# Attention and feed-forward layer on one core: the output product in three float32r passes, the softmax division on ScalarE, evictions without a buffer between

## The chip, the cores and the metric

The kernel runs on one core of a Trainium2 chip. The metric is the device time of one execution in microseconds; three runs of the kernel before gave 1560.99, 1563.09 and 1563.77 us, so the median is 1563.09 us. A core has five engines that run beside each other, each with its own in-order queue: TensorE (PE in the profile, with its weight loads as PEld), VectorE (DVE), ScalarE (ACT), GpSimd (POOL) and SyncE (SP), which here issues all transfers. Matmul results land in PSUM, in tiles of one bank each; only VectorE and ScalarE take them out ("evict" them) here.

## The reference

All arrays are float32. `x` is (2, 1024, 512), there are 16 heads of width 128, and the hidden layer has 1365 columns.

```
def attn(x):                                  # 16 heads, d_head 128, causal
    q, k, v = (einsum('bsd,hed->bhse', x, W) for W in (W_Q, W_K, W_V))
    scores = einsum('bhse,bhme->bhsm', q, k) / sqrt(128)
    pattern = softmax(where(causal, -1e9, scores))
    z = einsum('bhsm,bhme->bhse', pattern, v)
    return einsum('bhse,hde->bsd', z, W_O)    # the output product
def ffn(x):                                   # w1, w3, w2 rounded to three values
    return einsum('bsh,dh->bsd', silu(x @ w1q.T) * (x @ w3q.T), w2q)
x = x + layernorm(attn(layernorm(x)))
x = x + layernorm(ffn(layernorm(x)))
```

## The kernel before, in words

**Number formats.** TensorE is used in two ways. A float32 matmul is one instruction in the program and leaves two records in the profile. A float32r matmul takes operands of reduced width and leaves one record. The projections to query, key and value keep float32 accuracy with float32r: each operand is split into three forms, `lead` (the value scaled and cut to float32r), `low` (what is left) and `diff`, and a product is made of three passes: lead by lead and low by low go to one PSUM tile (`main`), the form `diff` by `diff` to a second one. `combine` (L414) then computes `main * (T12 + 1) - diff` with T12 = 4096. Weights arrive raw and are split on the core: `lead_and_low` (L394, ScalarE and GpSimd) and `difference_form` (L403, VectorE). Scores (L509), values (L572) and the output product (L478) use plain float32 matmuls.

**Loops.** The attention walks over 32 heads `n` (16 for each of two batches). Two heads make a pair `g` with `j` = 0 (even head) and 1 (odd head). Each head has eight steps `i`, one for each tile of 128 queries. In a step the main loop (L658 to L727) records, in this order: filler matmul groups from a table `fill`, the values of a finished block of two query tiles (`values`, L562), weight preparation, and the scores and softmax of the query tile that is three steps ahead (`look`, `AHEAD = 3`). The fillers are: query and key projections of the next head in steps 3 to 6; value projections of the next pair in steps 0, 1, 5 and 7 of odd heads; and in even heads the eight output units of the pair before (`output_units`, L472), one for each tile of 128 tokens, at steps 0, 1, 1, 3, 5, 7, 7, 7.

**Softmax of a tile** (`scores`, L504): matmuls to `s_ps` (two buffers), causal minimum and negated maximum on VectorE (L514, L518), exponent with row sum on ScalarE (L525), reciprocal on VectorE (L530), multiplication by it on VectorE (L531), two copies that separate the 16-bit halves on GpSimd (L536), a transposing transfer (L541), and, a step or more later, a copy to `pt` on VectorE (`join`, L557). Then `values` multiplies `pt` with `v_sb`, and ScalarE copies the result to `zT` (L579).

**PSUM.** Four banks (`ps_m`) serve projections, values, output units, transposes and the hidden layer in turn; two tiles of two banks (`ps_s`) serve the scores. An output unit takes one `ps_m` tile and two matmuls, and VectorE adds it to `acc` (L486; the first pair of a batch copies it, L484).

**What sets the order.** A scheduler turns the recorded order into one queue for each engine. `behind(...)` and `issue_after` hold marked work back until a named instruction has been placed. An engine never passes an instruction that waits.

**The end of the attention.** In the last head (n = 31) the fillers are four output units of the pair before, four `split_unit`s (L222, they load, normalise, transpose and split a tile for the feed-forward part) and two early hidden tiles of the feed-forward part (`early_hidden`, L645, `EARLY = 2`). After it come the last two values blocks and the last eight output units. `zL0` and `zL1` are separate buffers for the last pair. Then the feed-forward part runs hidden tiles (L285) and the product back (L765), and `load_t13` and `load_t2` fetch its weights; most of these weights lie where attention tiles lay.

Of the kernel before, what the change touches and what calls it, by code (L numbers as in the profile page):

```python
# [35 lines left out]
def sandwich_kernel(  # L36
# [16 lines left out]
    NC = D // P  # L53
    NT = S // P
    KB = 256
    QB = 512
# [248 lines left out]
    with ExitStack() as att:  # L305
# [5 lines left out]
        vpool = att.enter_context(tc.tile_pool(name="v", bufs=2))  # L311
        zpool = att.enter_context(tc.tile_pool(name="z", bufs=1))
        tpool = att.enter_context(tc.tile_pool(name="t", bufs=2))
        qpool = att.enter_context(tc.tile_pool(name="q", bufs=2))
# [61 lines left out]
        def load_raw(kind, n):  # L376

            if kind == 2:
                w, src = wpool.tile([P, NC, 2 * P], FP, name="wv", tag="vd"), wv[n % NP]
            else:  # L380
                w = wpool.tile([P, NC, P], FP, name="wqk", tag=("qd", "kd")[kind])
                src = (wq, wk)[kind][n % (2 * NP)]
            nc.sync.dma_start(w, src)
            wraw[kind, n] = w

        def load_output(g, tag):
            weights[3, g] = w = wpool.tile([P, 2, D], FP, name="wo", tag=tag)
            nc.sync.dma_start(w, wo[g % NP])

        def form(kind, name):  # L390
            shape = [P, NC, 2 * P if kind == 2 else P]
            return wpool.tile(shape, FR, name="qkv"[kind] + name)

# [20 lines left out]
        def combine(dst, main, diff, scale, shaped=lambda ps: ps):  # L414
            held = tpool.tile([P, TB], FP, name="held")
            nc.scalar.mul(held, main, scale * (T12 + 1.0))  # L416
            if scale == 1.0:
                nc.vector.tensor_tensor(
                    dst, shaped(held), shaped(diff), ALU.subtract
                )  # L420
            else:
                nc.vector.scalar_tensor_tensor(
                    dst, shaped(diff), -scale, shaped(held), ALU.mult, ALU.add
                )
# [47 lines left out]
        def output_units(g):  # L472
            b, pr = divmod(g, NP)

            def unit(t):
                ps = ps_m.tile([P, TB], FP, name="mm")
                for j in range(2):
                    nc.tensor.matmul(  # L478
                        ps, lhsT=zs[g, t // QT][:, j, ts(t % QT, P)],
                        rhs=weights[3, g][:, j, :],  # L480
                        start=(j == 0), stop=(j == 1),
                    )
                if pr == 0:
                    nc.vector.tensor_copy(acc[:, t, :], ps)  # L484
                else:
                    nc.vector.tensor_tensor(acc[:, t, :], ps, acc[:, t, :], ALU.add)  # L486

            return [lambda t=t: unit(t) for t in range(NT)]
# [15 lines left out]
        def scores(n, i):  # L504
# [25 lines left out]
            nc.vector.reciprocal(ri, rs)  # L530
            nc.vector.tensor_scalar(p_sb[:, :L], p_sb[:, :L], ri, None, ALU.mult)  # L531

# [29 lines left out]
        def values(n, m):  # L562

            g, j = divmod(n, 2)
            qb, half = divmod(m, 2)
            if j == 0 and half == 0:
                name = f"zT{qb}" if g < G - 1 else f"zL{qb}"
                zs[g, qb] = zpool.tile([P, 2, QB], FP, name=name)
            ps = ps_m.tile([P, TB], FP, name="mm")
            for kt in range(2 * m + 2):  # L570
                c0 = max(0, kt - 2 * m) * P
                nc.tensor.matmul(  # L572
                    ps[:, c0:KB],
                    lhsT=proj[g, 2][:, kt, ts(j, P)],
                    rhs=pts[n, m][:, kt, c0:KB],
                    start=(kt == 0),
                    stop=(kt == 2 * m + 1),
                )
            nc.scalar.copy(zs[g, qb][:, j, ts(half, KB)], ps[:, :KB])  # L579

# [61 lines left out]

        EARLY = 2

        def early_hidden(f):  # L645
            def pair():
                return [wpool.tile([P, TB], FR, name="qk"[f] + n) for n in "al"]

            hidden(0, 0, f, lambda: tpool.tile([P, TB], FP, name="held"), pair)

# [7 lines left out]
        for n in range(N):  # L658
# [18 lines left out]
            if j == 0 and g > 0:  # L677
                outs = output_units(g - 1)
                put((0, 1, 1, 3, 5, 7, 7, 7) if g < G - 1 else (0, 1, 3, 7), outs)
            if n == 2 * (NP - 1):  # L680
                units = [lambda t=t: block_unit(1, t) for t in range(NT)]
                put((4, 5, 5, 6, 6, 6, 7, 7), units)
            if n == 2 * NP + 1:
                put(sorted(2 * list(range(NT))), middle_units(0, xpool))
            if n == N - 1:
                splits = [lambda t=t: split_unit(0, 0, t, xpool) for t in range(QT)]
                put((0, 1, 2, 3), splits)
                put((1, 2, 3, 4), outs[QT:])
                put((6, 7), [lambda f=f: early_hidden(f) for f in range(EARLY)])
            for i in range(NT):  # L690
                idx = n * NT + i
                with behind("turn", of=idx + 1):
                    if n + 2 < N and i > 5:
                        load_raw(i - 6, n + 2)
                    if j == 0 and g + 1 < G and i == 1:
                        load_raw(2, g + 1)
                    if j == 1 and g < G - 1 and i == 2:
                        load_output(g, "wo")
                    if n == N - 1 and i == 0:
                        load_output(g, "vl")  # L700
                    if n == N - 1 and i < EARLY:
                        name = ("va", "vd")[i]
                        load_t13(i, wpool.tile([P, 2, D], FR, name=name))
                todo = fill[i]
# [7 lines left out]
                with behind("max", "half", "exp", of=idx + 1):  # L712
                    if n + 1 < N and i in (2, 3):
                        difference_form(i - 2, n + 1, EVERY)
                    if n + 1 < N and i in (1, 2):
                        lead_and_low(i - 1, n + 1, EVERY)
                    if j == 0 and g + 1 < G and i in (3, 4):
                        lead_and_low(2, g + 1, (FRONT, BACK)[i - 3])
                    if j == 0 and g + 1 < G and i in (5, 6):
                        difference_form(2, g + 1, (FRONT, BACK)[i - 5])  # L720
                look(idx + AHEAD)
# [12 lines left out]
    with ExitStack() as ffn:  # L734
# [6 lines left out]

        load_t13(EARLY, wpool.tile([P, 2, D], FR, name="wo"))
        t2 = [tpool.tile([P, D], FR, name=f"t2_{f}") for f in range(NF)]
# [70 lines left out]
        for f in range(NF):  # L814
            load_t2(f)
            if f > EARLY:
                load_t13(f, tpool.tile([P, 2, D], FR, name=f"t13_{f}"))
        middle = middle_units(1, xpool)
        for n, (b, tb, f) in enumerate(steps):
# [5 lines left out]
            if end and f == NF - 4:  # L825
                ffn_hidden(*steps[n + 2])
                ffn_hidden(*steps[n + 3])
            elif n + 2 < len(steps) and not (end and f == NF - 3):
                ffn_hidden(*steps[n + 2])
# [55 lines left out]
```

## Time and profile before

| | |
|---|---|
| median of three runs | 1563.09 us |
| profiled execution, its own time | 1561.59 us |
| its span (first to last instruction) | 1559.8 us |
| granted TensorE clock | 0.994 |
| output product (L478), 512 records | 232.6 us busy |
| softmax multiplication on VectorE (L531), 256 | 138.1 us busy |
| eviction copies to `held` on ScalarE (L416), 192 | 113.7 us busy |
| adding output units to `acc` (L486), 112 | 74.7 us busy |
| attention, about | 0 to 1311 us of the span |

Busy times are the union of an engine's records, so a busy engine may still have work that is stretched or pipelined: the records of matmuls that follow each other overlap, and the time from one start to the next is shorter than a record. For the cost of a matmul the length of a run of equal matmuls, divided by their number, is what counts. A "wait" names the engine and line that waited, what ended the wait, the sum in us, how often, and the longest. In the table of stages each engine has its busy time and, in brackets, its instructions.

### The profile page before, as it was taken

The page shows a single profiled execution, that of the slowest core. Times are in us where ns is not written, and L with a number is a line of the kernel's source. Part 1 is how long each engine was busy: PE and PEld are TensorE (multiplying, and loading weights), DVE is VectorE, ACT ScalarE, POOL GpSimd, SP SyncE. Part 2 cuts the span into 40 slices and gives each one's busy share as a digit, 9 for nine tenths or more (in the row PEclk, how much of TensorE's full clock was granted, in tenths as well). Part 3 has the DMA queues.
Part 4 walks back from the last instruction along what each step waited for, and adds up shares of the span by engine and source line. Part 5 has one row for each costly group of instructions (what it writes and reads, how often), then busy time and mean ns, then how long its engine had stood idle before and what let it go on. Part 6 is the DMA issues. An engine that isn't in the chain of part 4 may idle for free. (4 is left out here: it accounts for less than half of the span.)

```text
span 1559.8 us, 20141 instructions
## 1 busy us (share of the span) xinstructions
PE 1523.6 (98%) x6822; PEld 1143.9 (73%) x6822; DVE 1129.5 (72%) x2115; ACT 538.3 (35%) x1116; POOL 574.0 (37%) x685
## 2 busy tenths in 40 slices
PE   5999999999999999999999999999999999999997
PEld 4876868686868686677677777777777776888885
DVE  5787777777777878789887777777777784744343
ACT  4332323333334334333333333333333341433333
POOL 4434343433333546544454444444453330010010
PEclk9999999999999999999999999999999999999999
DMA  2374555555545455556655555555554476110100
GB/s 88 80 151 111 113 108 114 112 115 107 121 105 124 98 124 122 131 115 158 169 115 115 115 115 115 115 115 115 108 102 88 75 167 195 55 55 0 41 28 27
DMA packets 357615, 164.91 MB, mean 106 GB/s; under 512 B 311092, under 2 KB 324404, under 8 KB 357512
## 3 DMA queue, kind: packets, MB, share of 16 engines
q1 hardware_dynamic: 357512, 163.62, 45.8%
q8 instruction: 54, 0.88, 0.2%
q14 instruction: 49, 0.40, 0.1%
HBM read 73.39 MB, written 14.68 MB: 56 GB/s over the span
## 5 line engine op out<-in xcount | busy, mean ns | idle before, releaser
L536 POOL COPY half<-p_sb 128x640 uint16<-128x640 uint16 (+7 forms) x512 | 343.8, 700 | 712.9 <-DVE p_sb L531 371.7
L525 ACT ACTIVATE p_sb<-s_ps,nm 128x128 f32<-128x128 f32 (+7 forms) x256 | 189.9, 742 | 591.9 <-DVE nm L518 570.6
L509 PE MATMUL s_ps<-k,q 128*128 128x512 f32 (+3 forms) x768 | 290.1, 486 | 0.3 <-ACT p_sb L525 0.3
L572 PE MATMUL mm<-pt,v_sb 128*128 128x256 f32 (+1 forms) x1280 | 272.4, 360 | 5.9 <-DVE pt L557 3.5
L572 PEld LDWEIGHTS mm<-pt,v_sb 128*128 128x128 f32 x1280 | 239.9, 191 | 47.5 <-issue 8.2
L557 DVE COPY pt<-halfT 128x256 uint16<-128x256 uint16 (+7 forms) x256 | 248.2, 970 | 3.1 <-DMA halfT<-half 3.1
L478 PE MATMUL mm<-wo,zT 128*128 128x512 f32 x480 | 218.7, 592 | 0.0
L509 PEld LDWEIGHTS s_ps<-k,q 128*128 128x128 f32 x768 | 132.6, 191 | 92.4 <-issue 86.2
L518 DVE TENSOR_REDUCE nm<-s_ps 128x1 f32<-128x128 f32 (+7 forms) x256 | 193.5, 756 | 7.3
L514 DVE TENSOR_TENSOR s_ps<-s_ps,causal 128x128 f32<-128x128 f32 x256 | 75.6, 295 | 147.3 <-PE s_ps L509 147.1
L459 PE MATMUL mm<-va,xb 128*128 128x256 f32 x512 | 158.3, 309 | 0.0
L478 PEld LDWEIGHTS mm<-wo,zT 128*128 128x128 f32 x480 | 90.6, 189 | 92.3 <-issue 79.7
L416 ACT ACTIVATE held<-mm 128x512 f32<-128x512 f32 x192 | 113.7, 592 | 101.0 <-PE mm L459 66.1
L531 DVE TENSOR_SCALAR p_sb<-p_sb,ri 128x128 f32<-128x128 f32 (+7 forms) x256 | 138.1, 539 | 10.0 <-DVE ri L530 0.5
L459 PE MATMUL mm<-vd,xb 128*128 128x256 f32 x512 | 144.9, 283 | 0.3 <-DVE acc L486 0.3
L459 PE MATMUL mm<-vl,xb 128*128 128x256 f32 x512 | 144.6, 282 | 0.0
L285 PE MATMUL mm<-xb,t 128*128 128x512 f32 (+1 forms) x512 | 122.5, 392 | 0.0
L435 PE MATMUL mm<-xb,qa 128*128 128x512 f32 x256 | 120.9, 472 | 1.4 <-ACT xb L365 1.4
L435 PE MATMUL mm<-xb,ka 128*128 128x512 f32 x256 | 112.6, 440 | 0.0
L285 PEld LDWEIGHTS mm<-xb,t 128*128 128x128 f32 (+1 forms) x512 | 93.0, 183 | 21.4
L435 PE MATMUL mm<-xb,ql 128*128 128x512 f32 x256 | 102.9, 402 | 2.5 <-DVE xb L367 2.5
L459 PEld LDWEIGHTS mm<-vl,xb 128*128 128x128 f32 x512 | 97.8, 191 | 6.7 <-issue 3.6
(127 smaller groups left out, 2171.7 us busy)
## 6 DMA issues: line engine op xcount, KB each, us to landing
wqk<-wq SPq DMA_DIRECT2D x32, 256.0 KB, 3.5
wqk<-wk SPq DMA_DIRECT2D x32, 256.0 KB, 3.4
wv<-wv SPq DMA_DIRECT2D x16, 512.0 KB, 3.9
wo<-wo SPq DMA_DIRECT2D x16, 512.0 KB, 3.9
xt<-x SPq DMA_DIRECT2D x32, 256.0 KB, 3.2
raw<-w SPq DMA_DIRECT2D x30, 256.0 KB, 3.3
tern<-raw SPq DMA_DIRECT2D x30, 256.0 KB, 2.7
t<-tern SPq DMA_DIRECT2D x24, 256.0 KB, 5.5
```

The costliest lines, as they stand in the source:

```text
L285: nc.tensor.matmul(ps[:fl, :], lhsT=t[:, c, :], rhs=bl[k][:, c, :], start=(c == 0 and k == 0), stop=(c == NC - 1 and k == 1),)
L416: nc.scalar.mul(held, main, scale * (T12 + 1.0))
L435: nc.tensor.matmul(main, lhsT=forms[f][0][:, c, :], rhs=forms[f][1][:, c, :], start=(c == 0 and f == 0), stop=(c == NC - 1 and f == 1),)
L459: nc.tensor.matmul((main, main, diff)[f][:, ts(t, 2 * P)], lhsT=forms[f][0][:, c, token], rhs=forms[f][1][:, c, :], start=(t == 0 and c == ...
L478: nc.tensor.matmul(ps, lhsT=zs[g, t // QT][:, j, ts(t % QT, P)], rhs=weights[3, g][:, j, :], start=(j == 0), stop=(j == 1),)
L509: nc.tensor.matmul(s_ps[:, ds(k0, kl)], lhsT=proj[n, 0, i // QT][:, ts(i % QT, P)], rhs=proj[n, 1, k0 // TB][:, :kl], start=True, stop=True,)
L518: top = nc.vector.tensor_reduce(nm, s_ps[:, :L], axis=AX.X, op=ALU.max, negate=True)
L525: e = nc.scalar.activation(p_sb[:, :L], s_ps[:, :L], AF.Exp, bias=nm, accum_out=rs)
L531: nc.vector.tensor_scalar(p_sb[:, :L], p_sb[:, :L], ri, None, ALU.mult)
L536: copy = nc.gpsimd.tensor_copy(half[:, ds(k * L, L)], words[:, :L, k])
L557: nc.vector.tensor_copy(words[:, 0 : i + 1, :, ts(il, P)], turned[:, 0 : 2 * (i + 1), :].rearrange("p (k t) q -> p t k q", k=2),)
L572: nc.tensor.matmul(ps[:, c0:KB], lhsT=proj[g, 2][:, kt, ts(j, P)], rhs=pts[n, m][:, kt, c0:KB], start=(kt == 0), stop=(kt == 2 * m + 1),)
```

## The change

It does the following.

- **Output product.** `values` no longer copies `z` once. It writes three float32r forms of it: `lead` on ScalarE, `low` on VectorE (both read PSUM) and `diff` on GpSimd. The weights W_O are loaded raw like the value weights (`load_raw` kind 3), regrouped on the host, and split on the core in steps 3 to 6 of odd heads. An output unit is six float32r matmuls to two `ps_m` tiles, `main` and `diff`, and two VectorE instructions: `acc = main * (T12 + 1) + acc`, then `acc = acc - diff`. (The first pair of a batch does the first of the two on ScalarE.)
- **Buffers.** `zT` and `zL` give way to four rotating buffers of each form (`ZB = 4`).
- **Softmax.** The multiplication by the reciprocal goes from VectorE to ScalarE.
- **Evictions.** `combine` lets ScalarE write `main` straight to the destination, and VectorE subtracts `diff` in place; the tile `held` and its pool go.
- **End of the attention.** All output units of pair 14 stand in head 30. Three of the four splits move from head 31 to steps 5 to 7 of head 30. Three hidden tiles instead of two (`EARLY = 3`) stand in steps 2, 4 and 6 of head 31; their weights are loaded in head 30. In the feed-forward part the weights of hidden tiles 5 to 7 go to the buffers of W_O's forms.

```diff
         def combine(dst, main, diff, scale, shaped=lambda ps: ps):
-            held = tpool.tile([P, TB], FP, name="held")
-            nc.scalar.mul(held, main, scale * (T12 + 1.0))
+            nc.scalar.mul(dst, shaped(main), scale * (T12 + 1.0))
             if scale == 1.0:
-                nc.vector.tensor_tensor(
-                    dst, shaped(held), shaped(diff), ALU.subtract
-                )
+                nc.vector.tensor_tensor(dst, dst, shaped(diff), ALU.subtract)
...
             def unit(t):
-                ps = ps_m.tile([P, TB], FP, name="mm")
-                for j in range(2):
-                    nc.tensor.matmul(
-                        ps, lhsT=zs[g, t // QT][:, j, ts(t % QT, P)],
-                        rhs=weights[3, g][:, j, :],
-                        start=(j == 0), stop=(j == 1),
-                    )
-                if pr == 0:
-                    nc.vector.tensor_copy(acc[:, t, :], ps)
-                else:
-                    nc.vector.tensor_tensor(acc[:, t, :], ps, acc[:, t, :], ALU.add)
+                main, diff = (ps_m.tile([P, TB], FP, name="mm") for _ in range(2))
+                for f in range(3):
+                    for j in range(2):
+                        nc.tensor.matmul(
+                            (main, main, diff)[f],
+                            lhsT=zs[g, t // QT, j][f][:, ts(t % QT, P)],
+                            rhs=weights[3, g][f][:, 2 * j : 2 * j + 2, :],
+                            start=(j == 0 and f != 1),
+                            stop=(j == 1 and f > 0),
+                        )
+                dst = acc[:, t, :]
+                if pr == 0:
+                    nc.scalar.mul(dst, main, T12 + 1.0)
+                else:
+                    nc.vector.scalar_tensor_tensor(
+                        dst, main, T12 + 1.0, dst, ALU.mult, ALU.add
+                    )
+                nc.vector.tensor_tensor(dst, dst, diff, ALU.subtract)
...
             nc.vector.reciprocal(ri, rs)
-            nc.vector.tensor_scalar(p_sb[:, :L], p_sb[:, :L], ri, None, ALU.mult)
+            nc.scalar.mul(p_sb[:, :L], p_sb[:, :L], ri)
...
-            nc.scalar.copy(zs[g, qb][:, j, ts(half, KB)], ps[:, :KB])
+
+            lead, low, diff = (w[:, ts(half, KB)] for w in zs[g, qb, j])
+            nc.scalar.mul(lead, ps[:, :KB], LEAD / T12)
+            nc.vector.scalar_tensor_tensor(
+                low, lead, -T12, ps[:, :KB], ALU.mult, ALU.add
+            )
+            nc.gpsimd.tensor_tensor(diff, lead, low, ALU.subtract)
...
-        EARLY = 2
+        EARLY = 3
...
             if j == 0 and g > 0:
                 outs = output_units(g - 1)
-                put((0, 1, 1, 3, 5, 7, 7, 7) if g < G - 1 else (0, 1, 3, 7), outs)
+                put((0, 1, 1, 3, 5, 7, 7, 7), outs)
...
+            splits = [lambda t=t: split_unit(0, 0, t, xpool) for t in range(QT)]
+            if n == N - 2:
+                put((5, 6, 7), splits)
             if n == N - 1:
-                splits = [lambda t=t: split_unit(0, 0, t, xpool) for t in range(QT)]
-                put((0, 1, 2, 3), splits)
-                put((1, 2, 3, 4), outs[QT:])
-                put((6, 7), [lambda f=f: early_hidden(f) for f in range(EARLY)])
+                put((0,), splits[3:])
+                put((2, 4, 6), [lambda f=f: early_hidden(f) for f in range(EARLY)])
...
-                    if j == 1 and g < G - 1 and i == 2:
-                        load_output(g, "wo")
+                    if j == 1 and i == 1:
+                        load_raw(3, g)
...
-                    if j == 0 and g + 1 < G and i in (3, 4):
-                        lead_and_low(2, g + 1, (FRONT, BACK)[i - 3])
-                    if j == 0 and g + 1 < G and i in (5, 6):
-                        difference_form(2, g + 1, (FRONT, BACK)[i - 5])
+                    at = g + 1 - j
+                    if at < G and i in (3, 4):
+                        lead_and_low(2 + j, at, (FRONT, BACK)[i - 3])
+                    if at < G and i in (5, 6):
+                        difference_form(2 + j, at, (FRONT, BACK)[i - 5])
```

## The prediction

> **What bounds the kernel now.** I read the page's busy shares first, then the stages, the chain that ended last, the groups with their idle times, and VectorE's timeline inside one even head. The page:
>
> ```profile
> PE 1523.6 (98%) x6822; PEld 1143.9 (73%) x6822; DVE 1129.5 (72%) x2115; ACT 538.3 (35%) x1116; POOL 574.0 (37%) x685
> ```
>
> A busy PE need not stream at its full rate, so the chain that ended last, with runs of equal matmuls:
>
> ```profile
> 787.83 5.15 PE mm L478 x12
> ...
> 1287.03 4.24 DMA halfT<-half
> 1292.66 5.20 PE mm L572 x16
> 1297.86 13.73 PE mm L478 x32
> 1311.59 3.67 PE mm L285 x16
> 1317.08 3.63 PE mm L285 x16
> ```
>
> L478 is the output product in float32: 13.73 / 32 = 0.429 us for each record of 512 columns, two records for each matmul. L285 is float32r at 512 columns with a fresh stationary operand each time: 3.65 / 16 = 0.228 us. In the middle of the attention the output units run at the same 5.15 / 12 = 0.429, so there TensorE streams without holes. The stages agree (two odd and two even heads in turn):
>
> ```profile
> 950.00:989.00 39.00, 39.00 (x211) 32.10 (x211) 28.04 (x54) 13.64 (x30) 16.09 (x20) 1.00 0.54 129
> 989.00:1028.00 39.00, 39.00 (x142) 25.68 (x141) 32.36 (x58) 12.05 (x28) 19.96 (x22) 1.00 0.47 102
> 1028.00:1067.00 39.00, 39.00 (x212) 32.12 (x211) 27.98 (x53) 13.75 (x30) 16.09 (x20) 1.00 0.55 124
> 1067.00:1106.00 39.00, 39.00 (x142) 25.73 (x141) 32.68 (x58) 12.05 (x28) 19.97 (x22) 1.00 0.47 101
> ```
>
> After the span the columns are PE, PEld, DVE, ACT, POOL. TensorE bounds both kinds of head; VectorE is second, with 28.0 us in an odd head and 32.4 in an even one, where the output units stand. The groups that the change touches:
>
> ```profile
> L478 PE MATMUL mm<-wo,zT 128*128 128x512 f32 x480 | 218.7, 592 | 0.0
> L486 DVE TENSOR_TENSOR acc<-mm,acc 128x512 f32<-128x512 f32 x112 | 74.7, 682 | 25.6 <-PE mm L478 25.4
> L422 DVE SCALAR_TENSOR_TENSOR q<-mm,held 128x512 f32<-128x512 f32 x64 | 43.6, 681 | 3.2 <-PE mm L440 3.2
> L407 DVE SCALAR_TENSOR_TENSOR vd<-vl,va 128x512 fp32r<-128x512 f32 x32 | 24.4, 764 | 2.4 <-POOL vl L401 2.4
> L531 DVE TENSOR_SCALAR p_sb<-p_sb,ri 128x1024 f32<-128x1024 f32 x32 | 23.9, 748 | 1.0
> L525 ACT ACTIVATE p_sb<-s_ps,nm 128x1024 f32<-128x1024 f32 x32 | 35.8, 1118 | 89.7 <-DVE nm L518 89.7
> ```
>
> **The change part by part.**
>
> *Output product on TensorE.* Removed: 128 units x 4 records x 0.429 = 219.6 us. Added: 128 x 6 x 0.228 = 175.1. Gain 44.5 us, all on the path, because L478 waits for nothing (0.0 idle) and the stages are full. Bounds: 3.63 and 3.67 us per 16 give 45.3 and 43.5. The Trainium skill ("FP8 and Floating Point Precision", TensorE Precision Notes) counts four passes for true float32, and "TensorE: Matmul & The Clock Gate" (Back-to-back issue gap) gives about 216 ns for a warm 512-column pass; four passes to three would then give an estimated 128 x 2 x 0.216 = 55 us. The float32r rows here run at 0.228, and the sum keeps 44.5.
>
> *VectorE, even heads.* Each unit now needs two evictions of about 0.68 us (rows L422, L486) where it needed one: +8 x 0.68 = 5.4 us a head. The low form of z is new, four a head, 256 columns out of PSUM; no row has it. Between 295 ns for 128 columns (L514, 75.6 us over 256) and 681 for 512 I take 0.42: +1.7. The softmax multiplication goes: 138.1 us over 32 heads, -4.3. So 32.4 + 2.8 = 35.2 us of VectorE against 39.0 - 8 x 0.348 = 36.2 of TensorE: 97%. *Odd heads:* -4.3, +1.7, and two half forms of W_O at 0.764: 28.0 - 1.1 = 26.9 of 39.0, with room.
>
> What does 97% cost? A unit fills two of the four `ps_m` banks instead of one, so a late VectorE stops TensorE sooner: three units at step 7 take six banks. VectorE's idle time in the even head from 989 to 1028 us is mostly waiting for TensorE:
>
> ```profile
> 993.39 0.30 DVE L514 TENSOR_TENSOR s_ps<-s_ps,causal 128x128 f32<-128x128 f32 x1 [1.35 <-PE s_ps L509]
> ...
> 1008.41 0.30 DVE L514 TENSOR_TENSOR s_ps<-s_ps,causal 128x128 f32<-128x128 f32 x1 [0.49 <-PE s_ps L509]
> ...
> 1026.34 0.69 DVE L486 TENSOR_TENSOR acc<-mm,acc 128x512 f32<-128x512 f32 x1 [0.77 <-PE mm L478]
> ...
> 1028.06 0.69 DVE L486 TENSOR_TENSOR acc<-mm,acc 128x512 f32<-128x512 f32 x1 [1.02 <-PE mm L478]
> ```
>
> Together 6.3 us, of which 0.75 waits for ScalarE's row sums. Waits for TensorE vanish when VectorE is late, so VectorE needs between 35.2 + 0.75 = 35.95 us (nothing lost against 36.2) and 35.2 + 6.3 = 41.5 (5.3 lost). Below nothing cannot be, since TensorE's own work takes the 36.2. At steps 1 and 2 the even head is tight already: from 993.39 VectorE has eleven us of work in a row. Laying the new order on these durations, the values group after the pair of units waits about 0.3 us for the first unit's bank, 0.9 when the slow form of L207 (1.68 us) lies before it; the triple just fits. I take 0.6 us for each of 15 even heads: **+9 us** (0 to 80), nearer the low end because nearly all of that idle time is TensorE's.
>
> *Middle of the kernel.* From 720 to 800 us the row statistics of batch 0 come on top: VectorE 70.6 of 80, PE idle 2.3. The two later even heads get the same load plus 2.8 us: **+2.5** (0 to 6).
>
> *Softmax division on ScalarE.* Priced by the exponent of the same width (1118 ns for 1024, 189.9 us over all 256), ScalarE goes from 538 to about 538 + 190 + 20 (leads of W_O, 32 x 0.62) + 10, half of the span. The chain of a tile gets longer by 1.118 - 0.748 = 0.37 us, by one eviction of 0.59 queued between exponent and product, and by GpSimd, which gets 128 z differences (half of L371's 1417 ns, 0.7 each) and 32 halves of W_O (1.35 each, L401). Cover: the copy to `pt` waits for its transfer only 3.1 us in the whole run, so the transposed tile lies ready and VectorE's turn gates it; I take **+2** (0 to 32: the fourth values block of each of 32 heads starts only some 1.5 us after its copy, and would pay about 1 us). Were that cover gone, values wait and all later PE work with them. "VectorE: DVE Perf Modes" (The perf-mode tier table) speaks against this move: one-source float32 work between SBUF tiles runs there at twice the normal rate, which agrees with 748 against 1118 ns. By that rule alone the move loses an estimated 52 us of engine time; by the stages it takes VectorE's 4.3 us a head away where they are scarce.
>
> *Evictions without `held`.* Same instructions, same durations: nothing. ScalarE must now find the destination free; its last reader (scores at the latest in step 4) precedes the projection on PE's own queue.
>
> *z in three forms, W_O on the core.* ScalarE's lead replaces the copy (370 ns). Transfers: one of 512 KB for each pair as before, a step earlier, on SP before a transposition; it waits for the last reader of the form whose buffer it takes, done a step before. Nothing, covered by two steps (9 us) before its use.
>
> *End of the attention.* Four units, three splits and their loads leave head 31, a hidden tile enters; TensorE's total is unchanged. Left behind the last score are 3.66 + 1.51 + 2.38 = 7.5 us of PE work instead of 11.2 (two hidden tiles, two values blocks), while the softmax of the last tile takes the same 14.5 us (from about 1278.1 to 1292.66). It loses the splits that held VectorE (a load from `mid` on the chain at 1270.96) and gains about 1 us on ScalarE, where the activation-table load and the SiLU of the third hidden tile stand before its product. The hole before the last values block, 3.2 us, becomes about 7: **+4** (0 to 8). The last eight units take 8 x 1.36 us of VectorE plus row statistics (0.69 each) against 11.0 of TensorE: **+1** (0 to 3). Six loads of hidden weights now wait behind those units on SP; they are needed 12 us later: nothing.
>
> Sum: -44.5 + 9 + 2.5 + 2 + 4 + 1 = -26 us. The profiled execution took 1561.6 us, 1.5 under the median, so it would take 1535.6; against the median I say **1537 us**.
>
> **The rivals.**
> - *Everything is hidden* but the end: 1563.1 - 44.5 + 3 = 1521. For it: VectorE's idle time is TensorE's. Against: 97% in lumps.
> - *Values wait for the longer softmax chain.* The 32 fourth blocks pay 1 us: 1537 - 2 + 32 = 1567; half of them, 1552. For it: 1.5 us of slack. Against: 3.1 us of transfer waits.
> - *VectorE becomes the bound of the even heads; the kernel gets slower.* If all 6.3 us of idle time stay, an even head takes 41.5 instead of 39.0: 15 x 2.5 = +38, less 2.8 for the last units, plus 9.5 of the other terms: 1608. It decides when a head loses over (44.5 - 9.5) / 15 = 2.3 us, so when 3.3 of the 6.3 us stay. For it: four banks, two for each unit. Against: an odd head has 12 us of room to catch up.
> - *The passes are no cheaper* with z as a fresh stationary operand: the pass would have to take 0.286 us. Against: L285 loads one for each pass too, in 188 ns beside the matmul.
>
> **How the numbers follow.** Main case (1526 to 1549) 0.60; all hidden (1517 to 1526) 0.13; values wait in part (1549 to 1562) 0.12; values wait fully, VectorE bound, or passes no cheaper (over 1562) 0.15. Range 1518 to 1564 leaves out some 0.02 below and 0.14 above. A measurement of this kernel tells 0.2%, 3 us, from no change: faster 0.84, the same 0.02, slower 0.14.
>
> **What would show it.** In the profile after: L473 pitch 0.228 us; even heads about 36.8 us long, odd ones 39; VectorE near 35 us in an even head; waits of PE on VectorE's evictions (L484, L487, z low) of about 10 us in all; a hole of some 7 us before the last values block. Wrong if waits of the values on `pt` appear in bulk, if an even head is longer than 39 us, or if ScalarE's product is late because evictions before it wait for TensorE.

## The result, and the profile after

The changed kernel is slower by 0.5%: 1569.62 us (1568.53 to 1570.43 in five runs) against 1562.2 us (1560.5 to 1563.77 in five), a ratio of 1.0047, 95% interval 1.0032 to 1.0062. The forecast was 1537 us, with 1564 as its upper end and a chance of 0.14 for slower.

At first sight the page after contradicts this. Here it is, engine by engine (busy us, share of the span, instructions):

```profile
PE 1493.4 (95%) x7078; PEld 1192.4 (76%) x7078; DVE 1177.0 (75%) x2131; ACT 745.4 (48%) x1424; POOL 733.3 (47%) x845
```

TensorE is busy for 30 us less than before, and the span is 8 us longer (1567.6 against 1559.8). So TensorE's work shrank and it waits more. Its work is close to the forecast: from start to start a pass of L473 takes 0.229 us (median of 768), and the sum of all matmuls, each at the median of its kind, fell from 1507.4 to 1465.4 us, by 42. The same sum of the gaps that really passed rose from 1540.5 to 1547.1. The difference of the two sums is time beyond the usual pitch: 33 us before, 82 after. So some 49 us of new waiting stand against 42 us of saved work.

The groups of after that answer to those shown of before (after the bar: busy us in all and mean ns of one, then the engine's idle time just before them and what ended it):

```profile
L473 PE MATMUL mm<-oa,za 128*128 128x512 f32 x256 | 95.5, 454 | 5.8 <-DVE acc L484 5.6 <-DVE acc L487 0.2
L473 PE MATMUL mm<-ol,zl 128*128 128x512 f32 x256 | 79.8, 393 | 0.0
L484 DVE SCALAR_TENSOR_TENSOR acc<-mm,acc 128x512 f32<-128x512 f32 x112 | 74.2, 681 | 0.8
L582 DVE SCALAR_TENSOR_TENSOR zl<-za,mm 128x256 fp32r<-128x256 f32 x128 | 53.5, 418 | 79.1 <-ACT za L581 78.7
L585 POOL TENSOR_TENSOR zd<-za,zl 128x256 fp32r<-128x256 f32 x128 | 112.4, 878 | 83.9 <-DVE zl L582 60.3 <-ACT p_sb L526 15.0 <-DMA halfT<-half 5.1
L558 DVE COPY pt<-halfT 128x2048 uint16<-128x2048 uint16 x32 | 52.8, 1651 | 1.1 <-DMA halfT<-half 1.1
L208 DVE SCALAR_TENSOR_TENSOR raw<-raw,scales,tmp 128x512 f32<-128x512 f32 x30 | 40.8, 1359 | 12.7 <-POOL tmp L204 12.7
L532 ACT ACTIVATE p_sb<-p_sb,ri 128x1024 f32<-128x1024 f32 x32 | 36.9, 1152 | 29.6 <-DVE ri L531 29.3
```

The new instructions cost what was estimated (0.681 us an eviction, 0.418 a low form, 1.152 for the widest division, priced at 1.118). Two old ones grew that the change does not touch: the widest copy to `pt` from 1387 to 1651 ns, the ternary difference L208 (L207 before) from 987 to 1359 ns. The kernel before:

```profile
L557 DVE COPY pt<-halfT 128x2048 uint16<-128x2048 uint16 x32 | 44.4, 1387 | 2.9 <-DMA halfT<-half 2.9
L207 DVE SCALAR_TENSOR_TENSOR raw<-raw,scales,tmp 128x512 f32<-128x512 f32 x30 | 29.6, 987 | 3.9 <-POOL tmp L203 3.9
```

And VectorE now waits 78.7 us for ScalarE's lead form of z. The list of waits shows who is late (us in all, times, longest). The kernel after:

```profile
DVE zl L582 <- ACT za L581: 78.7, 92, 6.9
DVE s_ps L515 <- PE s_ps L510: 25.2, 42, 2.6
PE mm L572 <- DVE acc L484: 14.5, 10, 4.0
PE mm L572 <- DVE pt L558: 7.2, 3, 3.4
```

The kernel before:

```profile
DVE s_ps L514 <- PE s_ps L509: 147.1, 139, 2.9
PE mm L572 <- DVE pt L557: 3.5, 2, 3.2
```

Before, VectorE waited 147.1 us for the scores; now 25.2, so it is late in many places, and TensorE's values group L572 waits for its evictions. Summed over the run by the engine that ended them, VectorE's waits for TensorE fell from 279 to 123 us, but those for ScalarE rose from 97 to 192 and those for GpSimd from 10 to 31. (A lead of z can be written only when its values group is done: of the 79 us of idle time ahead of L582, 23 pass before TensorE has ended that group.)

A stage table of one even and one odd head (from the fourth score tile of a head to that of the next; columns as before, at the end the granted clock, the DMA share and GB/s). The kernel before:

```profile
992.30:1033.80 41.50, 41.50 (x167) 28.49 (x167) 33.25 (x58) 12.77 (x29) 22.10 (x25) 1.00 0.49 109
1033.80:1070.70 36.90, 36.90 (x191) 29.56 (x190) 27.43 (x52) 13.04 (x29) 14.02 (x19) 1.00 0.53 121
```

The kernel after, the same heads:

```profile
993.60:1034.90 41.30, 39.43 (x181) 31.06 (x180) 35.10 (x63) 18.79 (x38) 25.00 (x29) 1.00 0.52 121
1034.90:1071.50 36.60, 36.60 (x193) 29.96 (x192) 28.88 (x51) 19.32 (x39) 22.10 (x25) 1.00 0.57 122
```

VectorE's busy time in the even head is 35.10 us; the forecast said 35.2. Yet the head is 41.30 us long, and not about 39.7 (41.50 less seven units of 0.348, of the eight, that fall in this stage, plus the 0.6 us that the forecast gave away). VectorE is idle for 6.2 us of it, and hardly because of TensorE (0.8 us): it waits 1.3 for `v_sb`, 1.0 for `za`, 0.8 for row sums and 0.6 for q and k, all ScalarE's, and 1.0 us for GpSimd's `tmp`.

By stretches of the span (starts of the fourth score tile of a head), after minus before in us. The forecast column spreads the terms on record over the stretches (0.348 for each output unit, 0.6 lost in each even head, 2.5 in the middle, 5 at the end); c3 is an experiment below:

| stretch | before | after − before | forecast | c3 − before |
|---|---|---|---|---|
| heads 0, 1 | 118.1 | +3.6 | 0 | +0.9 |
| heads 2, 3 | 78.6 | −1.3 | −2.2 | −2.5 |
| heads 4 to 13 | 393.0 | −4.1 | −10.9 | −13.2 |
| heads 14 to 19 | 245.9 | +4.8 | −4.0 | +4.0 |
| heads 20 to 27 | 313.4 | −3.5 | −8.7 | −7.6 |
| heads 28, 29 | 78.3 | +3.4 | −2.2 | −2.6 |
| head 30 to the end | 332.4 | +5.1 | 0 | +3.1 |

No single place took the gain: each stretch is between one and nine us above the forecast. The first one, heads 0 and 1, has no output units yet; why it is 3.6 us longer was not followed. Where a regular even head loses is seen on VectorE's timeline. Head 6, kernel after (start, us, instruction, and in brackets the idle time ahead of it):

```profile
308.20 0.16 DVE L531 RECIPROCAL ri<-rs 128x1 f32<-128x1 f32 x1
310.98 0.69 DVE L148 TENSOR_REDUCE part<-xt 128x1 f32<-128x512 f32 x1 [2.62 <-DMA xt<-w]
311.58 1.28 DVE L484 SCALAR_TENSOR_TENSOR acc<-mm,acc 128x512 f32<-128x512 f32 x2
312.78 1.28 DVE L487 TENSOR_TENSOR acc<-acc,mm 128x512 f32<-128x512 f32 x2
```

L148 is a side unit (work for the feed-forward part, spread over the attention's steps), a reduction for the ternary scales. It waits 2.62 us for its transfer while two output units lie finished in all four `ps_m` banks behind it. TensorE then stands 1.90 us ahead of the third unit. In head 28 it is the ternary difference. VectorE:

```profile
1152.02 4.70 DVE L208 SCALAR_TENSOR_TENSOR raw<-raw,scales,tmp 85x512 f32<-85x512 f32 x1
1156.64 1.27 DVE L484 SCALAR_TENSOR_TENSOR acc<-mm,acc 128x512 f32<-128x512 f32 x2
```

GpSimd at that time:

```profile
1150.82 2.34 POOL L398 TENSOR_TENSOR ql<-wqk,qa 128x512 fp32r<-128x512 f32 x1
1153.11 0.72 POOL L585 TENSOR_TENSOR zd<-za,zl 128x256 fp32r<-128x256 f32 x1
1153.78 1.17 POOL L537 COPY half<-p_sb 128x512 uint16<-128x512 uint16 x2
1154.91 1.26 POOL L398 TENSOR_TENSOR kl<-wqk,ka 128x512 fp32r<-128x512 f32 x1
```

The same instruction took 1.67 us in the kernel before. It ends 0.55 us after the last of GpSimd's row of instructions, and behind it TensorE has its longest wait but one of the whole run (the longest, 9.6 us, stands at the very start):

```profile
1157.37 1.19 PE L572 MATMUL mm<-pt,v_sb 128*128 128x256 f32 x2 [4.01 <-DVE acc L484]
```

The end behaved as forecast at one place and not at another. The chain of the last tile (start, us, step):

```profile
1292.36 0.45 ACT p_sb L532
1292.81 0.82 issue
1293.63 2.53 POOL half L537 x2
1296.15 0.03 POOL zd L585
1296.18 4.25 DMA halfT<-half
1300.43 0.02 issue
1300.45 1.32 DVE pt L558
```

TensorE waits 3.05 and 3.40 us for these last copies, 6.5 in all, against 3.2 in the kernel before; about 7 were forecast. But at 1333 us another hole opens. SyncE's queue of transfers (SPq) and TensorE after:

```profile
1318.68 0.80 SPq L274 DMA_DIRECT2D oa<-tern  x2
...
1325.81 1.00 SPq L231 DMA_DIRECT2D xt<-mid  x2
```

```profile
1333.12 0.41 PE L238 MATMUL trx<-ident,xt 128*128 128x128 f32 x2 [3.13 <-DVE xt L117]
```

The hidden weights that go into `oa`, `ol` and `od` wait for the last output units, and behind them on SP stand the loads of `mid` for the next split. In c0 below, whose hidden weights do not go there, TensorE has no such wait; it has one of 7.4 us for the last copy to `pt`.

### The profile page after: what moved, and what is told of

Same layout as the page of the kernel before. It is cut to its first block, busy times and chain, and to the rows that moved or that the text cites. A ratio compares the mean times of both kernels' runs of the same rounds, so it can differ in the third digit from the quotient of the medians.

```text
span 1567.6 us, 20845 instructions
## 1 busy us (share of the span) xinstructions
PE 1493.4 (95%) x7078; PEld 1192.4 (76%) x7078; DVE 1177.0 (75%) x2131; ACT 745.4 (48%) x1424; POOL 733.3 (47%) x845
## 5 line engine op out<-in xcount | busy, mean ns | idle before, releaser
L537 POOL COPY half<-p_sb 128x640 uint16<-128x640 uint16 (+7 forms) x512 | 352.2, 718 | 492.4 <-issue 288.6
L572 PE MATMUL mm<-pt,v_sb 128*128 128x256 f32 (+1 forms) x1280 | 278.3, 365 | 26.1 <-DVE acc L484 14.5
L572 PEld LDWEIGHTS mm<-pt,v_sb 128*128 128x128 f32 x1280 | 242.4, 193 | 65.8 <-DVE acc L484 17.0
L558 DVE COPY pt<-halfT 128x256 uint16<-128x256 uint16 (+7 forms) x256 | 276.0, 1078 | 1.2 <-DMA halfT<-half 1.1
L532 ACT ACTIVATE p_sb<-p_sb,ri 128x128 f32<-128x128 f32 (+7 forms) x256 | 198.1, 774 | 93.2 <-DVE ri L531 91.5
L585 POOL TENSOR_TENSOR zd<-za,zl 128x256 fp32r<-128x256 f32 x128 | 112.4, 878 | 83.9 <-DVE zl L582 60.3
L582 DVE SCALAR_TENSOR_TENSOR zl<-za,mm 128x256 fp32r<-128x256 f32 x128 | 53.5, 418 | 79.1 <-ACT za L581 78.7
L453 PEld LDWEIGHTS mm<-va,xb 128*128 128x128 f32 x512 | 97.7, 191 | 6.2 <-issue 1.9
L429 PE MATMUL mm<-xb,kl 128*128 128x512 f32 x256 | 101.9, 398 | 0.4 <-POOL kl L398 0.4
L473 PE MATMUL mm<-oa,za 128*128 128x512 f32 x256 | 95.5, 454 | 5.8 <-DVE acc L484 5.6
L453 PEld LDWEIGHTS mm<-vd,xb 128*128 128x128 f32 x512 | 97.7, 191 | 1.6 <-DVE zl L582 0.7
```

The source lines that it names most:

```text
L429: nc.tensor.matmul(main, lhsT=forms[f][0][:, c, :], rhs=forms[f][1][:, c, :], start=(c == 0 and f == 0), stop=(c == NC - 1 and f == 1),)
L453: nc.tensor.matmul((main, main, diff)[f][:, ts(t, 2 * P)], lhsT=forms[f][0][:, c, token], rhs=forms[f][1][:, c, :], start=(t == 0 and c == ...
L473: nc.tensor.matmul((main, main, diff)[f], lhsT=zs[g, t // QT, j][f][:, ts(t % QT, P)], rhs=weights[3, g][f][:, 2 * j : 2 * j + 2, :], star ...
L532: nc.scalar.mul(p_sb[:, :L], p_sb[:, :L], ri)
L537: copy = nc.gpsimd.tensor_copy(half[:, ds(k * L, L)], words[:, :L, k])
L558: nc.vector.tensor_copy(words[:, 0 : i + 1, :, ts(il, P)], turned[:, 0 : 2 * (i + 1), :].rearrange("p (k t) q -> p t k q", k=2),)
```

## The experiments

The traces leave three explanations. Theory A: VectorE's queue puts side instructions (L148, L208) ahead of the evictions of two or three output units, which fill all banks. Theory B: GpSimd's new work stretches VectorE's instructions. Theory C: the division on ScalarE lengthens the softmax chain.

### One part at a time, on the kernel before

The division alone (its edit below), and the evictions without `held` alone (the edit of `combine` shown in the change):

```
-            nc.vector.tensor_scalar(p_sb[:, :L], p_sb[:, :L], ri, None, ALU.mult)
+            nc.scalar.mul(p_sb[:, :L], p_sb[:, :L], ri)
```

> The kernel before with the softmax division alone moved to ScalarE. Theory A and the prediction's step (+2 us, VectorE's turn gates the copy): 1560 to 1566, with VectorE some 138 us shorter. Theory B: the same or a little faster. Theory C: the chain of 256 tiles is longer by up to 0.37 us and queues behind evictions, values wait on pt in bulk: 1572 to 1595.

> The kernel before with the evictions of combine without the buffer held, nothing else. The prediction's step (nothing): 1559 to 1565. Rival: ScalarE's product, which now waits for its destination's last reader, holds ScalarE's queue and with it the exponents: 1568 to 1590.

Measured: 1561.68 us, ratio 0.9996 (0.9986 to 1.0006), and 1561.13 us, 0.9995 (0.9986 to 1.0004). Neither part costs anything by itself that these runs can tell. Theory C falls for the kernel before: the longer chain does not show in the time. Nor does a shorter VectorE: its busy time fell from 1129.5 to 1013.0 us, and nothing was earned.

Then the product, and the rest piece by piece on top of it. These kernels only round z and W_O (W_O on ScalarE) and do not split them exactly. The edits in short:

```
 def unit(t):
+    main, diff = two tiles; passes f = 0, 1, 2 over rounded z and W_O
+    acc = main * 1.0 + acc;  acc = acc - diff        # two VectorE instructions
```

> The kernel before with the output product alone in three float32r passes of 0.228 us into two banks, and two evictions a unit. z and W_O are only rounded, not split (all three passes read the same operands), so the product is float32r's and not exact; no low or difference forms are made. Theory A (order on VectorE's queue, side instructions ahead of the evictions of step 1): stalls of 1.5 to 2 us in each of 15 even heads, 1562 - 44.5 + 15 x 1.8 + 4 = 1545 (1537 to 1555). Theory B (contention of GpSimd's new work with VectorE): that work is not here, so nearly the whole gain shows, 1520 to 1532. Theory C (the division on ScalarE): also absent, 1520 to 1532.

```
 nc.scalar.copy(lead, ps[:, :KB])
+nc.vector.scalar_tensor_tensor(low, lead, -1.0, ps[:, :KB], ALU.mult, ALU.add)
+nc.gpsimd.tensor_tensor(diff, lead, low, ALU.subtract)     # not in b7_no_zd
```

> As b3_passes, plus for each values group the low form on VectorE (256 columns out of PSUM) and the difference on GpSimd, both into scratch that nothing reads. Theory A: VectorE's 4 x 0.42 us a head only, 3 to 10 us over b3_passes. Theory B: copies to pt go from 970 to about 1080 ns on average and TensorE's stalls with them, 15 to 30 us over b3_passes. Theory C: as theory A.

> As b4_passes_forms (1565), without the 128 differences of z on GpSimd; VectorE's low forms stay. Theory B (GpSimd's new work stretches VectorE's copies and ternary operations): back to within 6 us of b3_passes (1544), 1545 to 1551. Rival D (what costs is the low form on VectorE: 53 us of its time, and VectorE's queue standing behind ScalarE's lead until the values group ends): 1557 to 1565.

> As b4_passes_forms, plus the softmax division on ScalarE. Theories A and B: VectorE loses 4.3 us a head where it is short, 3 to 20 us below b4_passes_forms. Theory C: the longer chain of a tile and the product's place on ScalarE's queue make values or VectorE late, 10 to 30 us over b4_passes_forms.

| kernel | us | ratio to before (95%) | step |
|---|---|---|---|
| b3: passes, two evictions | 1544.12 | 0.9884 (0.9870 to 0.9899) | −17.3 |
| b7: + low form on VectorE | 1552.25 | 0.9937 (0.9922 to 0.9951) | +8.1 |
| b4: + difference on GpSimd | 1565.44 | 1.0023 (1.0014 to 1.0032) | +13.2 |
| b5: + division on ScalarE | 1558.04 | 0.9977 (0.9968 to 0.9987) | −7.4 |

So the passes earn 17 and not 44.5 us: already with two banks and two evictions a unit, and W_O only rounded, 27 of it are lost. The low form costs 8 us. The difference of z, an instruction on an engine that is busy for 44% of the span, and whose result nothing reads in b4, costs 13 us. What it does to the ternary difference is seen in the groups. b7:

```profile
L207 DVE SCALAR_TENSOR_TENSOR raw<-raw,scales,tmp 128x512 f32<-128x512 f32 x30 | 32.9, 1095 | 6.5 <-POOL tmp L203 6.3
```

b4:

```profile
L207 DVE SCALAR_TENSOR_TENSOR raw<-raw,scales,tmp 128x512 f32<-128x512 f32 x30 | 40.3, 1343 | 9.0 <-POOL tmp L203 8.8
```

It takes 0.25 us longer on average, 30 times. VectorE's 2355 instructions are the same in both, and by the pages they are busy for 15.3 us more (1241.5 to 1256.8): 7.4 us here, 4.4 in the softmax multiplications of 512 columns, 2.2 in the copies to `pt` (267.3 to 269.5 us). So theory B's stretching is there, and as large as the cost; how much of it lies in TensorE's way no run separates. And the division, useless alone, is worth 7.4 us here, where VectorE has 108 us less to do (1148.7 us busy in b5): theory C falls here too.

What b5 still lacks of the changed kernel is W_O's exact split, the evictions without `held` and the new end. The first two and what is left of the end add some 8 us up to c0 below, which no run takes apart; nor does any run take a single part out of the changed kernel itself.

### The side units one step later

In these cuts the old lines stand left, the new ones right:

```
-        at = 0                                  +        at = 1
-            at += (1 - at) % 4 + 4              +            at += (2 - at) % 4 + 4
```

> As b5_passes_forms_div (1558), but all side units (scales, statistics of batch 1, ternary weights) run one step later, so that the ternary difference L207 and the reduction L147 stand behind the evictions of step 1's two output units on VectorE's queue and not ahead of them. Theory A (order): the stalls of 1.1 to 1.3 us at step 2 of some twelve even heads and the 4.2 us one at 1153 us mostly go: 1538 to 1548. Theory B (contention, amount of work): VectorE is as late one step on, 1555 to 1560.

> The kernel before with all side units one step later, nothing else. Theory A: there a unit has one eviction and one bank, VectorE waits for TensorE and not the other way, so the order of the side units costs little: 1556 to 1562. Rival (the side units' place costs the kernel before as much): 1535 to 1548.

Measured: b6 1533.26 us, 0.9819 (0.9804 to 0.9833), 24.8 us below b5; b8 1561.12 us, 1.0000 (0.9990 to 1.0009). The same edit is worth nothing in the kernel before and 25 us once a unit has two banks and two evictions.

With the exact forms of the changed kernel two versions were run: c0, its end nearer to that of the kernel before, and c3, that with the shift. (In both, W_O's forms also have a pool of their own, and the weights of hidden tiles 5 to 7 do not go to them. From the output units on, their lines stand five further down than in the kernel after: L489 is its L484, L577 its L572.)

```
-        EARLY = 3                               +        EARLY = 2
-            if n == N - 2: put((5, 6, 7), splits)
+            if n == N - 1: put((0, 1, 2, 3), splits)
```

> The changed kernel with its exact forms and its order of units, but with more of the end of the kernel before: the four splits in head 31 and two hidden tiles ahead of the end in place of three; all eight output units stay in head 30. Theory A: the new end is worth 0 to 5 us, so 1565 to 1570, and the stalls at step 2 stay. Rival E (the end is what made the changed kernel slower, since heads 30 and 31 and the tail take 5 us more than in the kernel before): 1558 to 1564.

> As c0_early2, with all side units one step later, as in b6_shift. Theory A (order): the gain of b6_shift over b5_passes_forms_div (25 us) shows here too, 15 to 28 us below c0_early2, so 1540 to 1552. Rival (W_O's forms on GpSimd and VectorE fill what the shift frees): within 10 us of c0_early2.

Measured: c0 1566.08 us, 1.0038 (1.0023 to 1.0053), so its end is worth some 2 to 4 us (3.5 by the medians, 2.3 by their ratios to the runs of the kernel before that were taken with each; the two intervals overlap); c3 1544.30 us, 0.9898 (0.9881 to 0.9914). c3 computes all that the changed kernel does, and beats both kernels. Its page, and VectorE at the place shown above (head 6):

```profile
PE 1488.6 (97%) x7078; PEld 1190.8 (77%) x7078; DVE 1172.3 (76%) x2131; ACT 744.4 (48%) x1422; POOL 710.8 (46%) x845
```

```profile
302.42 0.16 DVE L536 RECIPROCAL ri<-rs 128x1 f32<-128x1 f32 x1
302.48 1.29 DVE L489 SCALAR_TENSOR_TENSOR acc<-mm,acc 128x512 f32<-128x512 f32 x2
303.67 1.29 DVE L492 TENSOR_TENSOR acc<-acc,mm 128x512 f32<-128x512 f32 x2
...
308.02 0.67 DVE L148 TENSOR_REDUCE part<-xt 128x1 f32<-128x512 f32 x1
```

VectorE's busy time is 1172.3 us against 1177.0: nearly the same work, 25 us less time than the changed kernel. So the amount of VectorE's work alone cannot be the cause. What TensorE gained is seen in its waits for the evictions. c0:

```profile
PE mm L577 <- DVE acc L489: 14.8, 12, 4.0
PE mm L478 <- DVE acc L489: 4.8, 4, 2.0
```

c3:

```profile
PE mm L577 <- DVE acc L489: 0.7, 1, 0.7
PE mm L478 <- DVE acc L489: 2.1, 6, 1.0
```

With all smaller ones, TensorE's waits for evictions to `acc` fall from 21.1 to 5.4 us: 15.7 of the 21.8 us between the two kernels. What changed on VectorE is how long side instructions hold it in the even heads. Adding the duration of each L148 and L208 and the idle time just ahead of it, over heads 2 to 28: 55.1 us in the even heads of c0, 34.8 in those of c3, 20.3 less, beside a time that is 21.8 less. In the odd heads, which have room, it rose from 33.8 to 39.6. Two things make the difference: one step later the transfer for L148 has landed (its waits fall from 12.1 to 3.6 us), and the instance of the ternary difference that meets GpSimd's row of work falls into the odd head (15 of the 17 in even heads take 0.74 or 0.75 us, where c0 has 1.1 to 4.7).

### One unit a step

```
-                put((0, 1, 1, 3, 5, 7, 7, 7), outs)
+                put((0, 1, 3, 4, 6, 7), outs[1:7])     # unit 0: step 7 of the odd head before
+                                                       # unit 7: step 0 of the odd head after
```

> The changed kernel with its exact forms, but the output units one a step: unit 0 at step 7 of the odd head, units 1 to 6 at steps 0, 1, 3, 4, 6, 7 of the even head, unit 7 at step 0 of the next odd head (the kernel after: 0, 1, 1, 3, 5, 7, 7, 7). The end is nearer to that of the kernel before: the splits in head 31, two hidden tiles ahead of the end and not three. Theory A with lumps: no step has two units, the waits of the values group at step 2 and of the triple at step 7 go, and VectorE has 2.7 us less to do in an even head: 1540 to 1550. Theory B (VectorE stretched by GpSimd in all steps): 1558 to 1568.

c2 is c1 with the side units one step later:

> As c1_spread, with the side units one step later as in b6_shift. Theory A: with one unit a step the side instruction ahead of it costs little, so 0 to 5 us below c1_spread. Theory B: the same as c1_spread.

d3 is c3 with the eighth unit alone moved:

```
-                put((0, 1, 1, 3, 5, 7, 7, 7), outs)
+                put((0, 1, 1, 3, 5, 7, 7), outs)       # unit 7: step 0 of the odd head after
```

> c3_shift with the eighth output unit at step 0 of the next odd head in place of step 7, so that step 7 has two units and not three. Steps 7 and 0 of an even head lose about 0.7 us more than the passes would give in eight or more heads: 1534 to 1541 if the triple is what costs them. Rival (the unit meets a value unit there, two banks each, as in c1_spread): 1543 to 1550.

Measured: c1 1569.94 us, 1.0047 (1.0030 to 1.0063); c2 1561.40 us, 0.9998 (0.9989 to 1.0008); d3 1543.52 us, 0.9878 (0.9862 to 0.9895), not told apart from c3. Spreading the units did not help, and the shift is worth 8.5 us there, not 22 to 25. Yet TensorE's waits for evictions to `acc` are nearly gone (2.9 us in c1, 0.2 in c2, against 21.1 in c0), so two units in one step had made them; others took their place, such as the values group's for ScalarE's eviction of k (4.3 us in c1, 6.8 in c2). In the program's order the unit meets a query or key unit in steps 3, 4 and 6, which takes two banks too. The waits for k point there; no run shows that this is why c2 stays 17 us above c3.

### Is it the place on the queue?

c3 with one more VectorE instruction in 15 even heads, a reduction that nothing reads, ahead of or behind the evictions of step 1:

```
+        for n in range(2, N, 2):
+            side[n * NT + 0].append(spare)      # d2, d5: n * NT + 1
```

> c3_shift (1544) with one more VectorE instruction in each of the 15 even heads from head 2 on: a reduction of 1024 columns of x that nothing reads (about 1.3 us), issued ahead of the evictions of step 1's two output units, where the ternary difference stood in the changed kernel. Theory A (the place on VectorE's queue): the stall at step 2 comes back, 15 x 0.8 to 1.3 us, so 1556 to 1564. Rival F (what the shift helped by is the time at which GpSimd's comparison and the transfers run, not VectorE's order): 1544 to 1549, as in d2_spare_behind.

> As d1_spare_ahead, with the same 15 reductions one step later, behind those evictions. Theory A: 1544 to 1550, less than half of what d1_spare_ahead loses. Rival F, and a rival in which only VectorE's amount of work counts: the same as d1_spare_ahead.

> As d1_spare_ahead (1552), with each of the 15 reductions over 2048 columns and not 1024 (about 2.3 us in place of 1.2), ahead of the evictions of step 1: as long as the ternary difference with its wait and its stretching, or the reduction with its wait for a transfer, held VectorE there in the changed kernel. Theory A, refined (an even head has some slack there, 0.5 to 1 us; beyond it every us that VectorE is held ahead of those evictions is a us of TensorE): 15 x 1.0 to 1.2 us more than d1_spare_ahead, 1566 to 1571, the changed kernel's time. Rival G (place matters little, amount does, as d1 against d2 could be read: 3 us apart): 1555 to 1560, near d5_long_behind.

> As d4_long_ahead, with the same reductions behind those evictions. Theory A, refined: 1550 to 1558, at least 10 us below d4_long_ahead. Rival G: within 5 us of d4_long_ahead.

| | 1.20 us each | 2.27 us each |
|---|---|---|
| ahead | d1 1552.49, +8.2 over c3 | d4 1555.19, +10.9 |
| behind | d2 1549.39, +5.1 | d5 1565.28, +21.0 |

Ratios to the kernel before: d1 0.9939 (0.9923 to 0.9956), d2 0.9916 (0.9902 to 0.9931), d4 0.9951 (0.9934 to 0.9968), d5 1.0019 (1.0010 to 1.0029). (By the ratios, which allow for the kernel before having been 1560.96 us beside c3 and 1561.68 and 1562.44 beside these, the four additions are 7.5, 4.4, 9.4 and 19.5 us.) Theory A as it stood falls: the long instruction costs twice as much behind the evictions as ahead of them. The rival by which only the amount counts falls too, since the two long ones lie 10 us apart. The traces say where TensorE waits: in d4 the values group for evictions to `acc` (9.7 us in 13 places, 0.7 in c3), in d5 the query and key projections for ScalarE's eviction of q (8.8 us in 10 places, 2.2 in c3). So it comes out in different places. What stands is that an even head has little slack on VectorE: wherever it is held there, 0.2 to 0.6 us of each us comes out as time (8.2 of 18.0, 5.1 of 18.1, 10.9 of 34.0, 21.0 of 34.1). The 20.3 us that the shift took out of the even heads would be worth only 5 to 13 us by that price; 21.8 were measured. Where the other 9 to 17 us come from stays open. The shift also moves GpSimd's comparisons and the transfers, and waits that were removed may be dearer than work that was added; no run separates these.

## Why the prediction was wrong

*Output product on TensorE, −44.5:* right in the main. The pitch is 0.229 us and TensorE's own work fell by 42 us. That all of it lies on the path held only as long as TensorE bounds every head; b3 earned 17.

*VectorE, even heads, +9:* the step that failed. Its sum was right (35.10 us busy where 35.2 was said). The share of 97% was not: the forecast's windows of 39.0 us are not heads. Cut at the heads, the even one before has 33.25 us of VectorE in 41.50; with the additions of seven units that is 35.4 of 39.1, or 91%. So there was more room than the forecast saw, and it was lost all the same. Wrong was what was made of the idle time: "Waits for TensorE vanish when VectorE is late, so VectorE needs between 35.2 + 0.75 = 35.95 us (nothing lost against 36.2) and 35.2 + 6.3 = 41.5". Of the waits for TensorE over half vanished (279 to 123 us in the whole run), but waits for ScalarE and GpSimd took their place (106 to 224 us), on an in-order queue: the low form waits for ScalarE's lead, L208 for `tmp`, L148 for a transfer. In the even head shown 6.2 us stayed idle, of 8.2 before. Measured, a regular even head loses 2.0 us (heads 4 to 13: 13.9 from the passes, 4.1 seen, five heads) or 1.9 (heads 20 to 27), and not 0.6. In these nine heads that is 12 us of the 36 by which the stretches exceed the forecast; heads 14 to 19 are 9 of it, heads 28 and 29, with the 4.01 us wait, 6, the end 5, heads 0 and 1 another 4. The third rival named the outcome, an even head that VectorE bounds because its idle time stays, with 2.3 us a head as the point where the kernel gets slower; the regular heads stopped just short of it, and the other stretches did the rest. The stretched ternary differences and copies were in no term.

*Middle, +2.5:* mis-sized. Heads 14 to 19 lost 13.1 us of 8.3 saved (forecast 4.3 lost); b3 lost 11.7 there, so the passes with two banks and two evictions a unit are enough for it. The shift of side units helps little there in the exact kernels (c0 is 4.5 us longer than the kernel before, c3 4.0).

*Division on ScalarE, +2:* wrong in sign, in our favour: 0 alone, −7.4 beside the other parts. Values do not wait on `pt` in bulk (7.2 us in three waits, 6.5 of them at the very end). The rule weighed there, from the Trainium skill, "VectorE: DVE Perf Modes" (The perf-mode tier table), agrees with the instruction's own time (1152 ns on ScalarE for 748 on VectorE) and does not decide the move.

*Evictions without `held`, 0:* right on the kernel before (b2).

*z in three forms, 0:* wrong. The low form's 1.7 us a head was in VectorE's sum, and b7 has +8.1 for it; the difference on GpSimd was priced only as a delay of the softmax chain, and b4 has +13.2 for it.

*End, +4 and +1, loads 0:* the hole was right in size (6.5 us in two waits; about 7 in one were forecast). "Six loads of hidden weights now wait behind those units on SP; they are needed 12 us later: nothing" failed for what stands behind them: loads of `mid`, and 3.1 us of TensorE. Undoing part of the new end gave some 2 to 4 us back (c0).

## What to carry to other kernels

When an engine that is not the bound is brought close to it, do not count its idle time as slack: list what it waits for, and ask which of those waits remain once it is late. Look then at side work on its queue that waits for a transfer or another engine; in this kernel, moving it by one step changed nothing where the engine had slack and earned 22 to 25 us where it had little (8.5 in another order of the units). And that GpSimd is idle does not make new work on it free: 128 instructions there cost 13 us.

## What the runs showed of the hardware

- VectorE's copies are longer while GpSimd is busy. Taking for each width of the copy to `pt` the fastest tenth as its base: in the kernel after, 68 copies with GpSimd busy for under a tenth of their time took 7 ns more than it, 122 copies with GpSimd busy for over half of it 285 ns more. In the kernel before it was 10 ns (166 copies) and 287 (68). The Trainium skill, "SBUF — State Buffer" (SBUF: two separate sides), says that VectorE, in some of its modes or with two SBUF inputs, and GpSimd contend for one port pair, which one of them gets for a whole instruction while the other is blocked. The longer copies agree that the two are in each other's way; that it is a lock they do not show.
- One ternary difference of 85 rows took 4.70 us in the kernel after, 1.67 in the kernel before and 0.74 in c3. GpSimd was busy for 4.35, 1.13 and 0 us of it. In the first case it ended 0.55 us after the last of four groups of GpSimd instructions that stood behind each other. The same section speaks of one instruction of the other engine that blocks; here the trace has VectorE's instruction open through several in a row.
